# Transposing attention probabilities with VectorE and DMA instead of TensorE, keys stored even first

## Chip, cores and metric

The kernel runs on one core of a Trainium2 chip. The metric is the device time of one execution in microseconds (us), the median of several runs. The engines are named as in the profile: PE is TensorE's matmul and PEld its weight load, DVE is VectorE, ACT is ScalarE, POOL is GpSimd, SP is SyncE, which here only issues DMAs.

## The reference

The input is eight sequences of 512 tokens with 256 features, in float32. Each goes through a layer norm, a two-layer transformer of local attention and a gated feed-forward, half of its output added; then a recurrence over the tokens; then the same norm and transformer again. All of it is float32. What the change touches is the attention:

```python
def local_attention(q, k, v):
    ...
    bk, bv = (look_around(bk), look_around(bv))
    ...
    sim = jnp.einsum('bhwid,bhwjd->bhwij', bq, bk)
    ...
    mask = (i < j) | (i > j + WINDOW) | (j == -1)
    sim = jnp.where(mask, -jnp.finfo(sim.dtype).max, sim)
    attn = jax.nn.softmax(sim, axis=-1)
    out = jnp.einsum('bhwij,bhwjd->bhwid', attn, bv)
    return out.reshape(b, h, n, d)
```

There are 8 heads of 64 features. A window is 128 queries; they see the keys of their own window and of the one before it. The mask leaves each query its own key and the 128 before it. The first window has no window before it.

## The kernel before

**Tiles and loops.** `sequence(b)` lays out the work of one sequence. It calls `attention` and `feed_forward` four times each (two passes, two layers), with the recurrence in between. Each attention loops over four windows `w` of 128 tokens, and within a window over two groups `g` of four heads. So there are 8 x 4 x 4 = 128 windows and 256 groups.

**One window.** `h.turn` (L665) transposes the tokens, `qk` (L717) and `v` (L804) project them, VectorE and GpSimd apply the rotary tables, and `qk.turn` (L828) transposes queries and keys into `qT` and `kT`. Then, for each group:

- `sc` (L868) makes the scores, with queries on the partitions and keys along the free dimension. Queries 0 to 63 see 192 keys, queries 64 to 127 see 192 keys that begin 64 later; the first window has 128 keys.
- `least` (L911, VectorE) adds the mask, writes `pr` and finds the minimum of the negated scores; `exp` (L923, ScalarE) makes exponentials and their sum, one head at a time. `recip` (L936 or L938) and `shares` (L944) divide by the sum, two heads at a time, on VectorE or GpSimd.
- `pr.turn` (L970) transposes the probabilities on TensorE, 64 x 64 at a time, into PSUM, since `po` needs the keys on the partitions. `pr.copy` (L629, the line of every plain copy) brings them into `prT`.
- `po` (L1007) multiplies them with the values; `po.copy` and `po.add` (L1051) write `oT`.

After both groups `py` (L1058) projects the window's output and adds it to `x`. In the feed-forward, `hs.shift` issues two or three DMAs for each window on SP (L1085, L1086, L1088) that move `x` from SBUF to SBUF with half of the features shifted by one token; `h2T` and `gate` (L1151) and `down` (L1242) are its large matmuls.

**Order.** The order of instructions is fixed when the program is built. Every piece of work is a node with its engine or a choice of engines, a cost in ns, the nodes it depends on, and the buffers that it takes and frees. `Scheduler.run` repeatedly puts down the node that could start first by these costs. The table `EARLY` advances or delays kinds of nodes, and `VARIED` varies the choice in stretches of 5000 ns of the plan. Up to three sequences (`lane`) are under way at once, so that one sequence's attention lies beside another's feed-forward. Where a node has two engines, the plan chooses. A node's `tail` is the time after its end at which its result counts as there; for DMAs it stands for the transfer.

Each engine executes its instructions in this order and waits at each for semaphores. SP's queue is one of them: a DMA that waits holds up those behind it. The buffers around the change are six of `pr` (two heads each) and two of `prT` (one group each).

Of the kernel before, what the change touches and what calls it, by code (L numbers as in the profile page):

```python
# [15 lines left out]
P = 128  # L16
# [9 lines left out]
GATE = 64  # L26
NH1 = 2 * NFC * P + GATE + REM
DS = 64
# [4 lines left out]
NLV = 7  # L33


def shape_constants():
# [18 lines left out]
    key = j + i // DH * DH  # L55
    amask = np.where((key > i + P) | (key < i), -NEG, 0.0)
    j = np.arange(P)[None, :]
    amask = np.concatenate([amask, np.where(j > i, -NEG, 0.0)], 1)
# [56 lines left out]
def t_pool(n, spread=False):  # L115
# [6 lines left out]
    "XT6": 200,  # L122
    "_full_quad": 850,
    "_full_rows": 350,
    "_quad_full": 400,
    "_quad_rows": 450,
    "_rows_full": 500,
    "_rows_quad": 650,
    "_table": -250,
    "base.x": -700,  # L130
    "base.y": 50,
    "base.z": -550,
    "below": -250,
    "block": 1000,
    "bx": 500,
    "bx.copy": -450,
    "bx6": 1000,
    "bx6.copy": -1000,
    "cross.mask": 2000,
    "down": -300,  # L140
# [4 lines left out]
    "gram": -50,  # L145
    "gram.copy": -750,
    "h.copy": -1650,
    "h.edge": 2100,
    "h.turn": 200,
    "h2T": -800,  # L150
    "hn": 350,
    "hn.turn": 250,
    "hs.rstd": -1350,
    "hs.stats": 100,
    "hs.zero": -400,
    "k.scale": 2350,
    "keys": -200,
    "keys.copy": -300,
    "kq": 5100,
    "kq.copy": -1000,  # L160
    "last": 200,
    "last.gelu": -650,
    "least": -250,
    "norm 0": 100,
    "norm 1": 400,
    "ones": 2100,
    "po": 3300,
    "po.add": 50,
    "po.copy": 100,
    "pr.copy": -250,  # L170
    "pr.turn": 150,
# [3 lines left out]
    "qk.add": -100,  # L175
    "qk.copy": 100,
# [3 lines left out]
    "qk.swapped": 2800,  # L180
    "qk.turn": 5050,
    "recip": 950,
    "remains": 650,
    "rest": -200,
    "rope": -2950,
    "sc": 2350,
    "sequence 4": 350,
    "shares": -50,
    "start": 1000,
    "tv": 2350,  # L190
    "u": 5500,
    "u.copy": -100,
    "v": -50,
    "value": 150,
    "w": 4650,
    "w.add": 350,
    "x.ffn": 200,
    "x.rstd": -1900,
    "x.scale": -500,
    "x.stats": 500,  # L200
    "xbx": 2650,
    "xbx.t": 500,
    "xbx6": 1000,
    "y": 300,
    "z.rstd": -400,
    "z.scale": 50,
    "z.stats": 5600,
    "zT": -450,
    "zero": -1000,
    "zn.rstd": -1850,  # L210
    "zn.scale": -350,
    "zn.stats": -500,
    "zn.turn": 4500,
# [6 lines left out]
    11539, 59206, 52431, 7169, 51312, 47193, 35081, 54701, 2496, 7793, 6049, 56177, 10364, 34536,  # L220
    8294, 4310, 20154, 19168, 52227, 29170, 16540, 21667, 50441, 20648, 28762, 21176, 51225, 49241,
    45956, 34971, 21009, 28142, 19477, 38168, 5557, 12352, 7023, 53196, 6017, 32604, 32616, 33833,
    43497, 35592, 8, 9511, 36946, 21011, 40384, 28542, 18616, 35469, 46717, 3648, 49052, 34713,
    26816, 29204, 8404, 4647, 15343, 36844, 570, 21424, 12355, 42492, 50428, 45178, 54350, 17920,
    13395, 135, 39989, 44533, 2549, 22957, 29261, 17027, 29544, 14357, 27402, 53285, 13020, 11910,
    26247, 40152, 22117, 30422, 46544, 22999, 49636, 47593, 30197, 3179, 35589, 32132, 42056, 18356,
    57054, 3385, 45135, 14935, 20770, 32612, 13353, 15733, 35692, 48376, 37702, 12678, 33060, 54960,
    27803, 54969, 53369, 31335, 34476, 36715, 13, 17472, 3933, 49344, 40320, 43761, 51808, 53819,
    30473, 58888, 28378, 53574, 53586, 34808, 30271, 11754, 5097, 46663, 4587, 12477, 2842, 20974,
    22949, 16164, 56345, 59752, 37818, 42810, 36514, 28003, 38920, 15614, 32190, 14889, 45329,  # L230
    56333, 3909, 22135, 44005, 49596, 54630, 11534, 50699, 55304, 13694, 14380, 32785, 48251, 51975,
    59596, 39815, 34672, 26684, 43342, 49501, 38504, 13035, 9055, 59153, 49831, 29616, 8451, 2950,
    5921, 10921, 22426, 31491, 10417, 40901, 35295, 21598, 37874, 47623, 56332, 58977, 50639, 51395,
    14345, 21523, 1611, 59581, 38356, 9024, 8797, 9600, 33490, 20077, 18908, 39770, 12624, 0, 51302,
    12996, 28627, 14230, 30261, 45539, 33994, 58844, 55888, 53070, 40769, 41472, 42381, 21824,
    25505, 26825, 37644, 26704, 31501, 49830, 52837, 21763, 24330, 27631, 47626, 31160, 32421,
    20990, 43125, 47451, 26149, 56263, 41669, 38285, 29128, 53275, 59120, 363, 15861, 23553, 38689,
    16, 59208, 8741, 59992, 24971, 2133, 29045, 13059, 56697, 49647, 42350, 46546, 32101, 980,
    58623, 42263, 42129, 58230, 58436, 55171, 53628, 11325, 17446, 17234, 26564, 12471, 44487,
    47246, 47905, 19512, 6228, 20309, 9884, 23474, 21539, 12749, 53397, 58236, 36711, 21477, 28615,  # L240
    11585, 23822, 4616, 960, 14012, 19245, 52408, 9606, 51939, 36194, 40143, 58969, 31327, 21363,
    19023, 20707, 24836, 4653, 46695, 9517, 40252, 20970, 35385, 8326, 20484, 11202, 51312, 9682,
    42952, 35195, 31373, 29093, 31724, 58081, 5082, 52637, 24194, 57630, 47639, 14785, 25712, 17698,
    27876, 35732, 43008, 43338, 18992, 8751, 5850, 25733, 15460, 31028, 26546, 27345, 36488, 44056,
    33295, 58977, 39749, 29184, 25121, 23756, 33811, 26536, 2260, 15160, 321, 39968, 25191, 31222,
    45604, 48604, 7672, 56893, 14684, 26720, 30312, 41919, 57072, 2421, 44875, 34765, 3604, 10279,
    45490, 35361, 22716, 21175, 46557, 5008, 49647, 1355, 7859, 39941, 43761, 4026, 49030, 9539,
    56965, 8358, 3988, 59899, 58021, 13265, 53954, 9411, 13889, 26300, 5547, 22515, 925, 22821,
    35389, 36309, 3233, 50482, 32683, 44192, 45433, 54698, 24152, 37273, 3714, 29516, 35158, 19134,
    31173, 30908, 46863, 51249, 42973, 41570, 7558, 58198, 43105, 36002, 53169, 27713, 15508, 57450,  # L250
    13353, 45327, 20959, 21312, 25608, 23768, 55045, 27334, 58634, 20168, 34664, 55665, 6316, 39132,
    11849, 10070, 18798, 46877, 11811, 49462, 58565, 1501, 28373, 7960, 55865, 56429, 52621, 1403,
    19983, 51522, 6552, 248, 6935, 6388, 4871, 4789, 20877, 23567, 24542, 21112, 42445, 40535,
    41468, 43567, 1697, 53106, 45256, 50440, 21162, 41824, 59524, 4758, 53095, 48105, 39745, 19805,
    15895, 4145, 51961, 47869, 41251, 39860, 1162, 32717, 5615, 59674, 43307, 49529, 2408, 1126,
    6903, 26424, 10998, 1128, 11983, 31727, 294, 20411, 37533, 25779, 45123, 39019, 22071, 17092,
    35693, 44717, 33182, 15800, 26669, 36844, 32178, 27395, 16355,
# [189 lines left out]
def macaron_kernel(ctx: ExitStack, tc: tile.TileContext, a: dict, out: bass.AP):  # L447
# [21 lines left out]
    def both_of(*vals):  # L469
# [14 lines left out]
        "pr": buffers("pr", 6, [P, 8 * DH]),  # L484
        "prT": buffers("prT", 2, [P, 4, 4, DH]),
# [9 lines left out]
        "s8": buffers("s8", 8, [P, 8]),  # L495
# [23 lines left out]
    def load_x(b, w=None):  # L519

        if not w:
            lane[b], first_x[b] = Val("lane"), Val("x")
        own = slice(0, NW) if w is None else slice(w, w + 1)
        if w == 0 and b >= 2:
            taken[b] = node("lane.take", (b, -NW - 1), "SP", 0.0, lambda e: None, takes=[lane[b], first_x[b]], tail=0.0)
        order[0] += 1
        n = node(
            "load.x",
            (-1, order[0]) if b < 2 else (b, (w or 0) - NW),
            "SP",  # L530
            1500.0 if w is None else 450.0,
            lambda e: dma(first_x[b].ap[:, own, :], a["x"][b].rearrange("(w p) d -> p w d", p=P)[:, own, :]),
            [taken[b]] if b in taken else [],
            takes=[] if w or b in taken else [lane[b], first_x[b]],
            uses=[first_x[b]] if w or b in taken else [],
            tail=3600.0 if w is None else 2900.0,
        )
        L["x", b] = [n] * NW if w is None else [*L.get(("x", b), []), n]
# [67 lines left out]
    def sequence(b):  # L606
# [62 lines left out]
        def attention(x, l, ready):  # L669
# [3 lines left out]
            n_qk = n_v = n_k = None  # L673
            for w in range(NW):
# [6 lines left out]
                    [ready[w], L["ident"]],  # L681
# [3 lines left out]
                )  # L685
                n_h = copy(
# [129 lines left out]
                qT, oT = Val("qT"), Val("oT")  # L816
# [4 lines left out]
                def turn(pts=pts, turned=turned):  # L821
                    out = both_of(*pts)
                    for i in (1, 0):
                        rot = turned[i][0].ap
                        for g in range(HEADS // 2):
                            for r in range(2):
                                rows, at = slice(r * DH, (r + 1) * DH), ((1 - i) * 4 + g) * DH
                                nc.tensor.transpose(  # L828
                                    out[:, r, at : at + DH], rot[rows, g * P : (g + 1) * P], ident[rows, rows]
                                )  # L830
# [6 lines left out]
                    takes=[*pts, kT[w], qT, oT],  # L837
# [21 lines left out]
                outs = []  # L859
                half = lambda r: slice(r * DH, (r + 1) * DH)  # L860
                for g in range(2):

                    sc, prT = [Val("ps"), Val("ps")], Val("prT")
                    prs, sts = [Val("pr"), Val("pr")], [Val("s8"), Val("s8")]
# [1007 lines left out]
```

## Time and profile before

| what | value |
|---|---|
| time, median of 3 runs | 2645.85 us (2645.41 to 2647.25) |
| span of the profiled execution | 2645.8 us |
| instructions in the profile | 77025 |
| mean granted TensorE clock | 1.000 |
| transposes of queries and keys (L828), busy | 89.0 us, 2048 records |
| `po` (L1007), busy | 198.1 us, 7168 records |
| table loads of ScalarE at L923, L1173, L1212 | 97, 72 and 26, 1283 ns each |
| DMA issues of `hs.shift`, L1085 / L1086 / L1088 | 128 / 128 / 96 |
| data moved by DMA | 44.69 MB, mean 17 GB/s |

The profile has one execution. Busy times are unions of an engine's records; matmuls are pipelined, so that records of TensorE overlap and the sum of their durations is larger than the busy time. A row of a group gives busy time, mean duration of one, then the idle time of the engine just before such instructions and what ended it. A float32 matmul leaves two records in some groups. Idle time of an engine that the others do not wait for costs nothing.

### The profile page before, as it was taken

The numbers are of one execution on the slowest core, as the hardware profiler recorded it, in microseconds if no ns is written. First come the engines' busy times: TensorE is split into PE (matmuls) and PEld (weight loads), VectorE is DVE, ScalarE is ACT, GpSimd is POOL, SyncE is SP. The second block draws the span as 40 slices with busy tenths as digits, with TensorE's granted clock in tenths as the row PEclk, the third lists the DMA queues.
The fourth block names the chain that finished last, engine by engine and source line by source line (L and its number), as shares of the span: only waits on it lengthen the run. The fifth ranks groups of instructions, "written<-read, shape, count | busy, mean of one in ns | idle before, by whom it ended". The sixth has DMA issues, their size and how long they took to land.

```text
span 2645.8 us, 77025 instructions
## 1 busy us (share of the span) xinstructions
PE 2610.2 (99%) x30608; PEld 1961.5 (74%) x30608; DVE 1968.5 (74%) x5827; ACT 1647.9 (62%) x4328; POOL 1434.5 (54%) x2045
## 2 busy tenths in 40 slices
PE   8999999999999999999999999999999999999998
PEld 5777777677777777777777777777777777776776
DVE  7776776867878767877877678787677867867755
ACT  4666667655667756665566666667557665555754
POOL 8655464546565455654644466375445754546533
PEclk9999999999999999999999999999999999999999
DMA  5000000000100000000000001000001000000000
GB/s 186 10 8 10 17 8 16 6 8 8 34 7 10 9 11 28 8 10 7 19 23 9 8 10 30 6 10 9 7 8 32 11 8 10 22 7 6 14 9 17
DMA packets 59231, 44.69 MB, mean 17 GB/s; under 512 B 8140, under 2 KB 56440, under 8 KB 58872
## 3 DMA queue, kind: packets, MB, share of 16 engines
q1 hardware_dynamic: 58872, 39.77, 5.0%
q8 instruction: 241, 3.95, 0.6%
q14 instruction: 118, 0.97, 0.1%
HBM read 18.79 MB, written 4.19 MB: 9 GB/s over the span
## 4 chain that ended last, share of the span: by engine, by line
PE 66%; DVE 3%; ACT 2%; POOL 1%; issue 1%; DMA 0%; SPq 0%; DVEq 0%; ACTq 0%; POOLq 0%
PE ps L1151 16%; PE ps L717 12%; PE ps L1242 7%; PE ps L804 6%; PE ps L1058 6%; PE ps L1007 4%; PE ps L868 4%; PE ps L970 3%; PE ps L665 2%; PE ps L828 2%; PE ps L1255 1%; PE ps L1387 1%; PE ps L1498 1%; PE ps L1483 1%; ACT pr L923 0%
## 5 line engine op out<-in xcount | busy, mean ns | idle before, releaser
L1151 PE MATMUL ps<-h2T,w 128*128 128x256 f32 (+1 forms) x2816 | 651.5, 381 | 3.2 <-ACT h2T L1129 1.4
L1151 PEld LDWEIGHTS ps<-h2T,w 128*128 128x128 f32 (+1 forms) x2816 | 518.6, 188 | 121.9 <-issue 29.4
L717 PE MATMUL ps<-wqkv,hT 128*128 128x512 f32 x1024 | 487.5, 601 | 1.9 <-DMA wqkv<-in_wqkv_dram 1.8
L923 ACT ACTIVATE pr<-pr,s 128x192 f32<-128x192 f32 (+1 forms) x1024 | 439.8, 432 | 64.5 <-DVE s L911 61.2
L753 POOL TENSOR_TENSOR st<-st,powc 128x8 f32<-128x8 f32 x256 | 439.6, 1717 | 21.3
L911 DVE CUSTOM_DVE_ANT_0 pr<-ps,amask,st 128x192 f32<-128x192 f32 (+1 forms) x1024 | 353.8, 395 | 31.1 <-PE ps L868 28.1
L944 POOL TENSOR_TENSOR pr<-pr,s 128x384 f32<-128x384 f32 (+1 forms) x313 | 243.1, 787 | 202.4 <-DVE s L936 188.3
L717 PEld LDWEIGHTS ps<-wqkv,hT 128*128 128x128 f32 x1024 | 185.5, 191 | 160.1 <-issue 140.6
L1192 DVE SCALAR_TENSOR_TENSOR gT<-ps,b,gl 128x256 f32<-128x256 f32 x320 | 152.0, 482 | 195.5 <-PE ps L1151 167.1
L1242 PE MATMUL ps<-w,gT 128*128 128x256 f32 x1280 | 291.4, 380 | 0.0
L1242 PEld LDWEIGHTS ps<-w,gT 128*128 128x128 f32 x1280 | 241.5, 190 | 48.6 <-issue 16.3
L736 ACT ACTIVATE tmp<-ps 128x512 f32<-128x512 f32 x256 | 152.1, 596 | 195.8 <-DVE rot L761 134.6
L938 POOL TENSOR_TENSOR s<-s,powc 128x2 f32<-128x2 f32 x174 | 122.8, 707 | 278.7 <-ACT pr L923 276.1
L629 ACT COPY prT<-ps 128x512 f32<-128x512 f32 (+1 forms) x322 | 157.8, 542 | 151.1 <-PE ps L970 148.4
L1058 PE MATMUL ps<-wo,oT 128*128 128x256 f32 x1024 | 243.4, 380 | 0.5 <-DVE s L911 0.3
L804 PE MATMUL ps<-wqkv,hT 128*128 128x512 f32 x512 | 240.6, 594 | 0.1
L761 DVE TENSOR_TENSOR rot<-ps,rt 128x512 f32<-128x512 f32 x256 | 175.1, 686 | 74.4 <-PE ps L717 65.3
L1058 PEld LDWEIGHTS ps<-wo,oT 128*128 128x128 f32 x1024 | 191.2, 190 | 46.9 <-issue 16.1
L1173 ACT ACTIVATE gl<-ps,b 128x256 f32<-128x256 f32 x320 | 142.9, 474 | 108.4 <-PE ps L1151 100.2
L1007 PE MATMUL ps<-prT,v 64*64 64x128 f32 (+1 forms) x7168 | 198.1, 247 | 3.3 <-DVE prT L629 2.1
L868 PE MATMUL ps<-kT,qT 64*64 64x128 f32 (+1 forms) x7168 | 193.1, 250 | 4.2 <-issue 2.1
L923 ACT ACTIVATION_READ_ACCUMULATOR pr<-pr,s 128x1 f32 x1024 | 193.7, 189 | 0.0
(124 smaller groups left out, 4420.7 us busy)
## 6 DMA issues: line engine op xcount, KB each, us to landing
hs<-x SPq DMA_DIRECT2D x128, 64.0 KB
hs<-x SPq DMA_DIRECT2D x128, 63.5 KB
base<-in_x_dram SPq DMA_DIRECT2D x8, 512.0 KB
out_dram<-base SPq DMA_DIRECT2D x32, 128.0 KB
w<-in_w_dram SPq DMA_DIRECT2D x6, 640.0 KB
x<-in_x_dram SPq DMA_DIRECT2D x28, 128.0 KB
wqkv<-in_wqkv_dram SPq DMA_DIRECT2D x2, 1024.0 KB
hs<-x SPq DMA_DIRECT2D x96, 0.5 KB
```

The source lines that it names most:

```text
L717: nc.tensor.matmul(pp.ap, hT[w].ap[:, c * P : (c + 1) * P], wqkv[:, c, i * INNER : (i + 1) * INNER], start=(c == 0), stop=(c == 1),)
L753: nc.gpsimd.tensor_tensor(ss, ss, powc[:, 0:HEADS], ALU.pow)
L761: nc.vector.tensor_tensor(heads(rot.ap), heads(pp.ap), tab, ALU.mult)
L804: nc.tensor.matmul(pv.ap, hT[w].ap[:, c * P : (c + 1) * P], wqkv[:, c, 2 * INNER : 3 * INNER], start=(c == 0), stop=(c == 1),)
L868: nc.tensor.matmul(sc[par].ap[half(c), k * 4 * DH + at : k * 4 * DH + at + keys.stop - keys.start], qT.ap[half(par), 2 * g + k, half(c)], ...
L911: nc.vector.tensor_tensor_reduce(out=pr(k, nj), in0=sc.ap[:, k * 4 * DH : k * 4 * DH + nj], in1=amask[:, 0:nj] if w else amask[:, 3 * DH : ...
L923: nc.scalar.activation(pr(k, nj), pr(k, nj), AF.Exp, bias=st.ap[:, k : k + 1], scale=-1.0, accum_out=st.ap[:, 2 + k : 3 + k],)
L944: (nc.vector if e == "DVE" else nc.gpsimd).tensor_tensor(both, both, st.ap[:, 4:6].unsqueeze(2).to_broadcast([P, 2, nj]), ALU.mult)
L1007: nc.tensor.matmul(po[r].ap[half(par), k * P + first : k * P + first + cols * DH], v[j].ap[half(r), hd * DH : (hd + 1) * DH], prT.ap[half( ...
L1058: nc.tensor.matmul(py.ap[:, 0:D], oT.ap[:, c, :], wo[:, c, :], start=(c == 0), stop=(c == INNER // P - 1))
L1151: nc.tensor.matmul(dst.ap[0:rows, 0 : 2 * P], w1[:, kc, col : col + rows], h2T.ap[:, kc, :], start=(kc == 0), stop=(kc == 1),)
L1242: nc.tensor.matmul(py.ap[:, 0:D], gT.ap[:, at : at + P], w2[:, c, :], start=(c == 0), stop=False)
```

## The change

The probabilities are no longer transposed by TensorE. VectorE transposes them in place, in blocks of 32 x 32, and DMAs then move the blocks from `pr` to `prT`, SBUF to SBUF. Four things go with it.

- The keys in `kT` are stored with the even keys of each 64 first, then the odd ones. `qk.turn` writes them so: position 32 v + k holds key 2 k + v. The mask is laid out in the same order by `paired`.
- `pr` is now one buffer for all 8 heads of a window, cut in 32-key blocks; there are three, taken at `qk.turn`. `prT` holds a whole window too. One `recip` serves the four heads of a group.
- After `shares`, one flip for each group transposes all blocks of four heads. When both groups are flipped, two `pr.move` nodes on SP issue the moves, 12 DMAs for a window and 6 for the first one. Each takes 32 partitions, two neighbouring 32-key blocks and 8 heads: partition k of block m goes to partition 2 k + m of a half of `prT`, which puts the keys back in order. `po` of both groups waits for them.
- The tables `EARLY` and `VARIED` have new numbers, which give all engines a new order; each sequence takes its lane by a node of its own; the `h.turn` of one attention depend on each other in order; the space kept for DMA descriptors is 256.

```diff
+BLK = 32
...
+def paired(j):
+
+    return j // DH * DH + j % BLK * 2 + j % DH // BLK
...
-    key = j + i // DH * DH
+    key = paired(j) + i // DH * DH
...
-    amask = np.concatenate([amask, np.where(j > i, -NEG, 0.0)], 1)
+    amask = np.concatenate([amask, np.where(paired(j) > i, -NEG, 0.0)], 1)
...
-    "po": 3300,
...
-    "pr.copy": -250,
-    "pr.turn": 150,
+    "pr.out": 1850,
...
-        "pr": buffers("pr", 6, [P, 8 * DH]),
-        "prT": buffers("prT", 2, [P, 4, 4, DH]),
+        "pr": buffers("pr", 3, [P, 3 * DH // BLK, HEADS, BLK]),
+        "prT": buffers("prT", 2, [P, 2, P // BLK, HEADS, BLK]),
...
-        "s8": buffers("s8", 8, [P, 8]),
+        "s8": buffers("s8", 5, [P, 16]),
...
-                    [ready[w], L["ident"]],
+                    [ready[w], L["ident"], n_h0],
...
+                                dst = out[:, r, at : at + DH]
                                 nc.tensor.transpose(
-                                    out[:, r, at : at + DH], rot[rows, g * P : (g + 1) * P], ident[rows, rows]
+                                    dst.rearrange("p (v k) -> p k v", v=2) if i else dst,
+                                    rot[rows, g * P : (g + 1) * P],
+                                    ident[rows, rows],
                                 )
...
-                    takes=[*pts, kT[w], qT, oT],
+                    takes=[*pts, kT[w], qT, oT, prs],
...
+                            pr = lambda hd=4 * g + 2 * k + par, nb=nb, prs=prs: prs.ap[:, 0:nb, hd, :]
+                            cut = lambda t: t.rearrange("p (m i) -> p m i", i=BLK)
...
+                            nc.vector.reciprocal(st.ap[:, 8:12], st.ap[:, 4:8])
...
+                            both = prs.ap[:, 0:nb, 4 * g + 2 * k : 4 * g + 2 * k + 2, :]
+                            by = st.ap[:, 8 + 2 * k : 10 + 2 * k].unsqueeze(1).unsqueeze(3).to_broadcast([P, nb, 2, BLK])
+                            (nc.vector if e == "DVE" else nc.gpsimd).tensor_tensor(both, both, by, ALU.mult)
...
-                    def turn_pr(pts=pts, prs=prs, w=w):
-                        for h in range(4):
-                            for n in range(2 if w else 1):
-                                for r in range(2):
-                                    lo = DH + h % 2 * 3 * DH + (n * P - r * DH if w else 0)
-                                    at = (h * 2 + n if w else h) * DH
-                                    nc.tensor.transpose(
-                                        pts[r].ap[:, at : at + DH],
-                                        prs[h // 2].ap[half(r), lo : lo + P],
-                                        ident[half(r), half(r)],
-                                    )
...
+                    def flip(prs=prs, nb=nb, g=g):
+                        own = prs.ap[:, 0:nb, 4 * g : 4 * g + 4, :]
+                        nc.vector.transpose(own, own)
+
+                    flips.append(dve("pr.flip", 60.0 + 1.1 * 4 * nj, flip, [*n_w, *flips], takes=[] if g else [prT], uses=[prs]))
+
+                def moves(q, w=w, prs=prs, prT=prT):
+                    for m in range(3 if w else 1 + q // 2):
+                        n, u = divmod(m + (q // 2 if w else 2), 2)
+                        dma(
+                            prT.ap[u * DH : (u + 1) * DH, n, q].rearrange("p h i -> p (h i)"),
+                            prs.ap[q * BLK : (q + 1) * BLK, 2 * m : 2 * m + 2].rearrange("k m h i -> k m (h i)"),
                         )
...
+                moved = [
+                    node(
+                        "pr.move",
+                        prio(),
+                        "SP",
+                        (6 if w else 2 + 2 * r) * 430.0,
+                        lambda e, r=r, moves=moves: [moves(q) for q in (2 * r, 2 * r + 1)],
+                        flips,
+                        uses=[prs, prT],
+                        tail=2300.0,
+                    )
+                    for r in range(2)
+                ]
...
+                            out = po[r].ap[half(par), k * P + first : k * P + first + cols * DH]
                             nc.tensor.matmul(
-                                po[r].ap[half(par), k * P + first : k * P + first + cols * DH],
+                                out.rearrange("p (q i) -> p q i", i=BLK),
                                 v[j].ap[half(r), hd * DH : (hd + 1) * DH],
-                                prT.ap[half(r), h, n : n + cols, :],
+                                prT.ap[half(r), n // 2, q : q + 2 * cols, hd, :],
...
-                        [*tps, *(vals[j] for j in blocks)],
+                        [*moved, *(vals[j] for j in blocks)],
...
-        for pr in pools["pr"]:
-            for edge in (slice(0, DH), slice(7 * DH, 8 * DH)):
-                nc.gpsimd.memset(pr[:, edge], 0.0)
...
-    nc = bacc.Bacc("TRN2", target_bir_lowering=False, num_devices=1)
+    nc = bacc.Bacc("TRN2", target_bir_lowering=False, num_devices=1, dynamic_dma_scratch_size=256)
```

## The prediction

> **What bounds the kernel now.** I read the page's busy shares and slices first, then the chain of work that ended last, then the groups of instructions with shapes kept apart, then the timelines of TensorE and of the DMA queue.
>
> ```profile
> PE 2610.2 (99%) x30608; PEld 1961.5 (74%) x30608; DVE 1968.5 (74%) x5827; ACT 1647.9 (62%) x4328; POOL 1434.5 (54%) x2045
> ...
> PE   8999999999999999999999999999999999999998
> ...
> PEclk9999999999999999999999999999999999999999
> ```
>
> TensorE is busy in 99% of the span at the full granted clock, in every slice alike. Of 2645.8 us it is idle in 35.6. By windows, 11.2 us of that lie in the first 100 us and 6.6 in the last 46; some 18 are left for the 2500 us between. So there is no wait to remove: only TensorE work can be saved.
>
> ```profile
> PE 66%; DVE 3%; ACT 2%; POOL 1%; issue 1%; DMA 0%; SPq 0%; DVEq 0%; ACTq 0%; POOLq 0%
> ```
>
> The chain says the same: other engines end a wait in 6% of it.
>
> ```profile
> L970 PE MATMUL ps<-sq,pr 64*128 64x64 f32 x3584 | 144.1, 225 | 3.1 <-DVE pr L944 0.7 <-POOL pr L944 0.7 <-DVE tmp L767 0.7
> L629 ACT COPY prT<-ps 128x512 f32<-128x512 f32 x239 | 131.1, 596 | 106.2 <-PE ps L970 103.5 <-ACT tttb L1378 0.8 <-ACT pr L923 0.7
> L629 DVE COPY prT<-ps 128x512 f32<-128x512 f32 x145 | 95.1, 685 | 35.2 <-PE ps L970 34.3
> L944 DVE TENSOR_TENSOR pr<-pr,s 128x384 f32<-128x384 f32 x148 | 87.7, 611 | 2.3 <-POOL s L938 0.6
> L629 ACT COPY prT<-ps 128x256 f32<-128x256 f32 x83 | 26.7, 386 | 44.9 <-PE ps L970 44.9
> L944 DVE TENSOR_TENSOR pr<-pr,s 128x256 f32<-128x256 f32 x51 | 23.2, 465 | 0.9
> L629 DVE COPY prT<-ps 128x256 f32<-128x256 f32 x45 | 17.3, 419 | 17.1 <-PE ps L970 17.0
> ```
>
> L970 is the transposition of probabilities that goes away; its copies stand on ScalarE and VectorE.
>
> **Removed from TensorE.** The 144.1 us of L970 overlap with their neighbours, because each matmul of 225 ns is started long before the last one ends. What the removal frees is the distance from start to start:
>
> ```profile
> 1035.37 2.32 PE L1242 MATMUL ps<-w,gT 128*128 128x256 f32 x10
> 1037.63 1.21 PE L970 MATMUL ps<-sq,pr 64*128 64x64 f32 x32
> 1038.67 0.66 PE L828 MATMUL ps<-sq,rot 64*128 64x64 f32 x16
> ...
> 1056.37 0.66 PE L970 MATMUL ps<-sq,pr 64*128 64x64 f32 x16
> 1056.95 3.29 PE L1151 MATMUL ps<-h2T,w 128*128 128x256 f32 x14
> ```
>
> 32 of them hold the engine from 1037.63 to 1038.67, 1.04 us; 16 before a full matmul, 0.58. At 0.55 us per 16 (34.4 ns each) 3584 give 123 us; the bounds are 32.5 ns (116 us) and 36.5 ns, the mean over all stretches of L970 up to whatever follows (131 us). A change between full-array and partial-array matmuls costs extra: the ten matmuls of L1242, 0.215 us apart elsewhere, hold 2.26 us here, 0.11 too many. I counted such changes in the order of instructions of both programs: 558 before, 563 after. The stretches with L970 often also hold L828, which remains, so nothing comes from there. 2645.8 - 123 = 2523.
>
> **Added to TensorE.** No matmul is added. The first matmuls of each window's `po` now wait for the semaphores of twelve DMAs instead of two copies; the order shows 835 waits that need an instruction of their own, 665 before, at 51 ns each in the trace: 170 x 51 ns = 9 us at most, nothing if they pass while matmuls drain. I take 4. The 1024 key transposes of L828 write every 32nd word of PSUM in turn. No row shows that; L828's 89.0 us for 2048 bound it: 0 to +44 us if the half concerned took twice as long. I take 0, by the plain L828 row, since the same words are written, only in another order.
>
> **VectorE.** It loses the copies (95.1 + 17.3 = 112.4), 120 of 338 reciprocals at 159 ns (19, one now serves four heads), 55 of its 148 large `shares` at 593 ns (33, the order puts them on GpSimd), and 28 of 157 additions at 694 ns (19). It gains 192 flips of 768 elements per partition and 64 of 512, an operation no row shows. Low end, by the copies: (685 - 419) / 256 = 1.04 ns per element, so 951 and 685 ns, 226 us in all. By `shares`, (611 - 465) / 128 = 1.14 ns, 1049 and 757 ns, 250 us. High end, if it ran at half the rate, 500 us. I take 235, nearer the copies (one input, one output). 1968.5 - 183 + 235 = 2020 us, 80% of 2523, against 74% now: no bound. ScalarE loses 157.8 us of copies and 28 of 195 table loads at 1283 ns, and stands near 1460 us; GpSimd loses 136 of 174 reciprocals and takes over `shares` and additions, and stays at 1433.
>
> [...]
>
> **The moves.** Each window (four 128-row blocks, two layers, two passes, eight sequences: 128) gets 12 DMAs, or 6 for the first block of each attention: 96 x 12 + 32 x 6 = 1344 of 64 KB, issued on SP. The nearest row is the shift of `hs`, also SBUF to SBUF:
>
> ```profile
> 401.97 0.51 SPq L1085 DMA_DIRECT2D hs<-x  x1
> 402.53 0.62 SPq L1086 DMA_DIRECT2D hs<-x  x1
> 403.20 0.94 SPq L1088 DMA_DIRECT2D hs<-x  x1
> ```
>
> One issue to the next takes 0.56 us at L1085 (64 KB) and 0.67 at L1086; the stores to DRAM (352 ns median) give 0.41. The packets of one L1085 begin 1.16 us after its issue and are all done at 1.50, over many engines at once; the 127 rows of L1086 go one after another, 23.5 ns apart, to 4.99 us. 64 packets of 1 KB take 46 to 53 ns each: 1344 x 64 x 50 ns / 16 = 270 us per engine, a tenth of the span. SP's issues, 1344 x 0.56 = 753 us and 128 shifts of 2.2, fill under half. So neither is a throughput bound.
>
> What can cost is lateness. All twelve moves of a window stand between its last flip and its first `po`: 12 x 0.56 = 6.7 us and 1.0 to land, 7.7. The program's own plan, which fixes the order, allows 12 x 0.43 + 2.3 = 7.5. By L1790's price it is 5.9, by L1086's 9.1. Between a window's last `sc` and its first `po`, the new order puts a median of 17.9 us of TensorE work (counted from the order, each matmul at its start-to-start time above). The steps between, each without queueing, are four `least` (1.7), the rest of the exponentials (0.9), `recip` and `shares` (1.0), the last flip (1.0) and the moves (7.7): 12.3 us. So the cover exists, but it is not large. Queued behind a waiting move on SP are the shifts: 86 times the order puts moves right after a shift, whose three issues hold SP for 2.2 us where the plan has 0.5. At 2.2 of 20.7 us per window a tenth of 128 windows meets one, for 1 us on average, half of it exposed: 6 us. Each DMA also waits for the one eight places ahead of it to land; 8 x 0.56 covers 1.5 us, not an L1086's 4.4, and that is in the same 1 us. At the start the first moves queue behind weight loads that keep the DMA engines full from 10 to 36 us: 0 to 10 us, I take 4. If the cover is gone, a microsecond of lateness costs 128 us.
>
> **The rest of the diff.** New tables of the plan set a new order of all work. Its worth is bounded by TensorE's idle time: the 18 us in the middle can be gained, the second rival is the loss; I take 0. The extra order among `h.turn` binds instructions of one engine, the memsets left out are twelve short ones of GpSimd at the start, and the smaller scratch space issues nothing: 0.
>
> **Sum:** 2645.8 - 123 + 4 + 6 + 4 = 2537 us. The runs' median, 2645.85, is the profiled span, so nothing is added around it.
>
> **The rivals.** First: flips at half rate (500 us). VectorE then stands at 2285 us, 90% of the span, and each window's path is 2 us longer; a quarter of it exposed gives 2537 + 64 = 2600. For it: nothing in the profile shows a transpose. Against: one-input rows run near 1.04 ns per element.
>
> Second, slower than before: SP's issues set the pace of each window. Lateness per window is 10.5 moves x (price - 0.43); fully exposed, 1344 x (p - 0.43) eats the 109 us from p = 0.51 on, half exposed from 0.59. At L1086's 0.67 and half exposed: 2537 + 161 = 2698. For it: the price of L1085 lies between these points. Against: the faster landing (1.0 for 2.3 planned) pays back 1.3 us of each window, and the plan drops the 3300 ns by which `po` was advanced, so `po` now yields to other ready work, which is slack.
>
> Third: the moves do not spread over the DMA engines, as L1086 does not. 64 packets at 46 ns in a row, 1344 times, is 3960 us. L1085's 128 rows spread; 32 and 64 rows are not shown. [...]
>
> Fourth: TensorE has the time but nothing ready to fill it, and idles it away: 2646.
>
> **How the numbers follow.** Forecast, 2505 to 2590: 0.70; its low end is 2645.8 - 131 and a little for a shorter wait elsewhere, its high end the 44 us of strided writes. Better than that, 0.03. Flips at half rate, 0.10. SP's pace, 0.13. No spread, 0.02. No change, 0.02. A change of 0.2% (5 us) is about what can be told from none here. Faster is 0.70 + 0.03 + 0.10 = 0.83, same 0.02, slower 0.15. The likeliest case gives 2537; a range of 2502 to 2620 takes in the half-rate flips and leaves the slower cases out.
>
> **What would show it.** TensorE still at 97% or more of a shorter span, L970 and the copies of `prT` gone, VectorE near 2020 us, flips near 0.95 us, moves 0.5 to 0.6 us apart on SP and landed within 2 us. Idle time of TensorE before `po`, released by DMA `prT`, beyond 15 us speaks for the second rival; a flip above 1.5 us for the first. I am wrong if TensorE's busy time does not fall by about 120 us.

## The result, and the profile after

The changed kernel takes 2729.34 us, the median of 4 runs (2729.08 to 2732.07), where the kernel before takes 2645.63 (2644.73 to 2647.25) beside it: a ratio of 1.0315, interval 1.030 to 1.033. It is slower by 84 us; the forecast was 109 us faster. The profiled execution has a span of 2727.3 us at a mean granted clock of 0.982.

First the busy shares and the slices of the changed kernel.

```profile
PE 2575.4 (94%) x27024; PEld 1893.8 (69%) x27024; DVE 2009.3 (74%) x5669; ACT 1479.3 (54%) x3999; POOL 1428.2 (52%) x1980
...
PE   7998999999999999999999999999999999999988
```

TensorE has 3584 records fewer, and yet its busy time fell by 34.8 us only (2610.2 before), while its share fell from 99% to 94%. The other engines are where the prediction had them: VectorE 2009 us (2020 foretold), ScalarE 1479 (1460), GpSimd 1428 (1433). The chain of work that ended last names what is new.

```profile
PE 75%; DMA 7%; SPq 6%; DVE 6%; ACT 3%; issue 2%; POOL 1%; DVEq 0%; ACTq 0%; POOLq 0%
```

DMA and SP's queue had 0% of the chain before; together they now have 13%. The groups, with shapes kept apart, say at which line TensorE waits.

```profile
L1009 PE MATMUL ps<-prT,v 64*64 64x128 f32 x3584 | 222.4, 296 | 98.9 <-DMA prT<-pr 78.8 <-issue 8.6 <-DVE s L923 4.3
...
L977 DVE STREAM_TRANSPOSE pr<-pr 128x768 f32<-128x768 f32 x192 | 185.8, 970 | 11.9 <-POOL pr L960 8.1
...
L977 DVE STREAM_TRANSPOSE pr<-pr 128x512 f32<-128x512 f32 x64 | 45.1, 706 | 3.1 <-POOL pr L960 1.0
```

L1009 is `po`. Its first form alone has 98.9 us of idle time ahead of it; 78.8 of them end when a move into `prT` lands. Of the kernel before, the same row:

```profile
L1007 PE MATMUL ps<-prT,v 64*64 64x128 f32 x3584 | 180.9, 275 | 3.3 <-DVE prT L629 2.1 <-ACT prT L629 0.8 <-issue 0.2
```

The flips at L977 cost 970 and 706 ns, 230.9 us in all.

Here is one window. First SP's queue, then TensorE, then all engines in three stretches of it (columns: length, then busy time of PE, PEld, DVE, ACT and POOL, each with its records, then PEclk, the granted clock in parts of full speed, the DMA engines' share, and GB/s).

```profile
1074.81 0.52 SPq L1087 DMA_DIRECT2D hs<-x  x1
1075.37 0.68 SPq L1088 DMA_DIRECT2D hs<-x  x1
1076.09 0.92 SPq L1090 DMA_DIRECT2D hs<-x  x1
1077.12 7.67 SPq L984 DMA_DIRECT2D prT<-pr  x12
```

```profile
1082.91 0.72 PE L840 MATMUL ps<-sq,rot 64*128 64x64 f32 x16
1085.83 2.91 PE L1009 MATMUL ps<-prT,v 64*64 64x128 f32 x61 [2.20 <-DMA prT<-pr]
1088.44 0.42 PE L882 MATMUL ps<-kT,qT 64*64 64x128 f32 x1
```

```profile
1080.00:1085.50 5.50, 3.63 (x30) 2.86 (x28) 2.02 (x5) 2.02 (x4) 1.27 (x1) 1.00 0.41 101
1085.50:1088.90 3.40, 3.07 (x73) 3.10 (x77) 0.85 (x2) 0.02 (x1) 0.00 (x0) 0.50 0.09 22
1088.90:1095.00 6.10, 6.10 (x49) 4.19 (x42) 4.41 (x22) 5.51 (x19) 2.23 (x4) 1.00 0.00 1
```

A shift holds SP for 2.3 us, then twelve moves go out in 7.67 us, 0.64 each; the last is out at 1084.79 and `po` starts 1.04 us later, at 1085.83, after 2.20 us in which TensorE had nothing. The semaphores show that its first matmul waits for the eleventh move, which lands at 1085.70; the twelfth lands only at 1086.31. Then a second cost appears that the forecast did not have: for the next 3.4 us the granted clock is 0.50, and `po` itself runs slowly (61 matmuls in 2.91 us; after the wait that ends at 1010.64, at full clock, 61 take 1.92). Between the first and the last matmul the clock is halved for 95.6 us (0 before).

A third change is small but everywhere: instructions that only wait for semaphores, between the matmuls of `po`, for the moves that are still to land. They stand in the stream of weight loads (PEld). The first line is of the kernel before, the second of the changed one (durations in ns: least, median, most).

```profile
L1007 PEldq EVENT_SEMAPHORE  x169: 51/51/51, 33.1 to 2607.3; - x169
```

```profile
L1009 PEldq EVENT_SEMAPHORE  x584: 51/51/3020, 39.8 to 2693.3; - x195
```

The account, from TensorE's records. A matmul holds the engine from its start to the next one's start; idle time is taken out of this and stands apart, counted from the first matmul to the last:

| part | us |
|---|---|
| L970 gone | -127 |
| TensorE's idle time, 23.4 to 141.3 (of it before `po`, 3.3 to 104.1) | +118 |
| matmuls in the half-speed stretches, against the same matmuls at the rate of before | +42 |
| the other matmuls, held longer (`po` +24, L840 +8, the rest in parts below 5) | +50 |
| sum (the spans differ by +81.5; the first matmul starts 1.6 us sooner) | +83 |

So all that L970 held is gone, and 210 us come back: waits, most of them for the moves, the halved clock after them, and matmuls held longer.

### The profile page after: what moved, and what is told of

It reads as the page before. It is cut to its first block, busy times and chain, and to the rows that moved or that the text cites. A ratio compares the mean times of both kernels' runs of the same rounds, so it can differ in the third digit from the quotient of the medians.

```text
span 2727.3 us, 71864 instructions
## 1 busy us (share of the span) xinstructions
PE 2575.4 (94%) x27024; PEld 1893.8 (69%) x27024; DVE 2009.3 (74%) x5669; ACT 1479.3 (54%) x3999; POOL 1428.2 (52%) x1980
## 4 chain that ended last, share of the span: by engine, by line
PE 75%; DMA 7%; SPq 6%; DVE 6%; ACT 3%; issue 2%; POOL 1%; DVEq 0%; ACTq 0%; POOLq 0%
PE ps L1153 20%; PE ps L728 13%; PE ps L1244 8%; PE ps L1009 7%; PE ps L1060 7%; PE ps L815 6%; SPq L984 5%; PE ps L882 5%; DMA prT<-pr 4%; PE ps L675 2%; DMA hs<-x 2%; PE ps L840 2%; DVE pr L923 1%; ACT pr L935 1%; PE ps L1389 1%
## 5 line engine op out<-in xcount | busy, mean ns | idle before, releaser
L1153 PE MATMUL ps<-h2T,w 128*128 128x256 f32 (+1 forms) x2816 | 655.6, 383 | 8.4 <-DVE gT L1194 3.4
L1153 PEld LDWEIGHTS ps<-h2T,w 128*128 128x128 f32 (+1 forms) x2816 | 519.4, 189 | 124.9 <-issue 21.7
L960 POOL TENSOR_TENSOR pr<-pr,s 128x384 f32<-128x384 f32 (+1 forms) x368 | 290.1, 807 | 418.7 <-DVE s L949 370.6
L728 PE MATMUL ps<-wqkv,hT 128*128 128x512 f32 x1024 | 490.8, 604 | 2.3 <-DMA wqkv<-in_wqkv_dram 2.1
L935 ACT ACTIVATE pr<-pr,s 128x192 f32<-128x192 f32 (+1 forms) x1024 | 439.1, 431 | 73.4 <-DVE s L923 67.4
L764 POOL TENSOR_TENSOR st<-st,powc 128x8 f32<-128x8 f32 x256 | 434.1, 1696 | 21.3
L1009 PE MATMUL ps<-prT,v 64*64 64x128 f32 (+1 forms) x7168 | 237.9, 265 | 104.1 <-DMA prT<-pr 82.9
L1009 PEld LDWEIGHTS ps<-prT,v 64*64 64x64 f32 x7168 | 210.1, 145 | 134.9 <-issue 76.4
L648 POOL TENSOR_SCALAR st<-st 128x1 f32<-128x1 f32 (+1 forms) x192 | 49.7, 259 | 390.8 <-DVE st L1101 226.9
L815 PE MATMUL ps<-wqkv,hT 128*128 128x512 f32 x512 | 245.7, 604 | 2.2 <-DVE tmp L778 2.2
L977 DVE STREAM_TRANSPOSE pr<-pr 128x768 f32<-128x768 f32 (+1 forms) x256 | 230.9, 904 | 15.0 <-POOL pr L960 9.1
L1060 PEld LDWEIGHTS ps<-wo,oT 128*128 128x128 f32 x1024 | 192.0, 191 | 54.1 <-issue 20.1
L639 ACT COPY oT<-ps 128x256 f32<-128x256 f32 x232 | 86.5, 373 | 235.7 <-PE ps L1009 233.3
## 6 DMA issues: line engine op xcount, KB each, us to landing
hs<-x SPq DMA_DIRECT2D x128, 63.5 KB
```

What stands on the lines that cost most here:

```text
L728: nc.tensor.matmul(pp.ap, hT[w].ap[:, c * P : (c + 1) * P], wqkv[:, c, i * INNER : (i + 1) * INNER], start=(c == 0), stop=(c == 1),)
L764: nc.gpsimd.tensor_tensor(ss, ss, powc[:, 0:HEADS], ALU.pow)
L815: nc.tensor.matmul(pv.ap, hT[w].ap[:, c * P : (c + 1) * P], wqkv[:, c, 2 * INNER : 3 * INNER], start=(c == 0), stop=(c == 1),)
L935: nc.scalar.activation(pr(), pr(), AF.Exp, bias=st.ap[:, h : h + 1], scale=-1.0, accum_out=st.ap[:, 4 + h : 5 + h],)
L960: (nc.vector if e == "DVE" else nc.gpsimd).tensor_tensor(both, both, by, ALU.mult)
L977: nc.vector.transpose(own, own)
```

## The experiments

Theory A: the moves come late because SP needs about 0.65 us for each, one after another, where the plan has 0.43; TensorE waits before `po`, and the halved clock and the semaphore instructions follow from that. Theory B, as the rival: what costs is in TensorE's own work, above all the key transposes that now write every 32nd word, or in the new order.

**Fewer moves of the same kind.** One move of three is kept in every full window; the rest of `prT` is cleared once at the start.

```diff
-                    for m in range(3 if w else 1 + q // 2):
+                    for m in [1] if w else [0]:
...
+        for t in pools["prT"]:
+            nc.gpsimd.memset(t, 0.0)
```

> The changed kernel in its order with 4 of 12 moves for each window (one for each block of 32 queries); the other probabilities are not moved, and prT is cleared once at the start. Theory A: 4 x 0.65 + 1.1 = 3.7 us against 7.5 planned, idle time before po under 15 us, the clock at full speed nearly throughout, 2530 to 2570 us, near what the removal of the transposes alone was worth. Theory B: above 2650 us.

2559.52 us (one run), span 2557.4. Its shares:

```profile
PE 2508.0 (98%) x27024; PEld 1847.0 (72%) x27024; DVE 2005.7 (78%) x5669; ACT 1475.7 (58%) x3999; POOL 1431.9 (56%) x1982
```

All instructions of the compute engines are those of the changed kernel (GpSimd has two clearings more), in the same order; only moves are missing. TensorE's idle time falls to 39.0 us, before `po` to 3.4, the half-speed time to 13.7. TensorE's busy time alone falls by 67 us though it does the same work: the clock and most of what `po` is held longer, too, hang on the moves. Theory A is right about the cause of the waits before `po`. B is left with the 18 us by which matmuls are still held longer than before (7 of them at L840), and with 16 us more of idle time elsewhere than before `po` (35.6 against 20.1).

**The same data in eight moves instead of twelve.** The score columns are laid out so that two pieces of 64 keys that go to the same partitions lie side by side, and travel as one DMA of 128 KB.

```diff
-        "prT": buffers("prT", 2, [P, 2, P // BLK, HEADS, BLK]),
+        "prT": buffers("prT", 2, [P, P // BLK, 2, HEADS, BLK]),
...
-                    for m in range(3 if w else 1 + q // 2):
...
+                    c = q // 2
+                    if w:
+                        dma(into(c, 0, 2), part(c, 2))
+                        dma(into(1 - c, c, 1), part(2 * (1 - c), 1))
...
```

> Same plan and order as the changed kernel, correct output, but a full window is moved in 8 DMAs instead of 12: the scores' columns and prT are laid out so that two 64-key pieces of one query block go in one DMA with 2 KB pieces. Theory A (the loss is lateness: SP needs 0.65 us for each move, 12 x 0.65 + 1.1 us to land = 8.9 us where the plan allows 7.5): 8 x 0.65 + 1.1 = 6.3 us, so TensorE's idle time before po falls from 104 us to under 30, the half-speed time of its clock from 98 us to under 40, and the time from 2729 to 2590 to 2630 us. Theory B (the loss comes from elsewhere in the change: semaphore waits on TensorE, strided writes of keys, VectorE's load, the new order itself): within 20 us of 2729. Should the price of an issue grow with its bytes, A would give some 2690 us.

2593.89 us, ratio 0.9803 (0.9786 to 0.9819): it beats both kernels. Its shares and its `po`, then the issues of its moves (L996 is the move of 128 KB, L997 that of 64 KB):

```profile
PE 2525.5 (97%) x27024; PEld 1858.1 (72%) x27024; DVE 2006.1 (77%) x5669; ACT 1476.7 (57%) x3999; POOL 1426.2 (55%) x1980
...
L1022 PE MATMUL ps<-prT,v 64*64 64x128 f32 (+1 forms) x7168 | 207.1, 249 | 22.5 <-DMA prT<-pr 13.6
```

```profile
L996 SPq DMA_DIRECT2D prT<-pr x384: 537/597/1544, 48.4 to 2556.1; - x192
L997 SPq DMA_DIRECT2D prT<-pr x384: 537/597/1810, 49.0 to 2556.7; - x192
```

Twice the bytes cost the same 597 ns of SP. So the price is one for each of these DMAs, and four DMAs fewer in a window are worth 135 us. Idle time before `po` falls from 104.1 to 22.5 us with the bytes unchanged. The bytes are not free in the transfer: by its semaphore, a move of 128 KB has landed 2.62 us after its issue began (median), one of 64 KB in the changed kernel 2.13.

**The strided writes alone.** The kernel before, with the keys even first in the key transposes only and the mask left as it was.

```diff
+                                dst = out[:, r, at : at + DH]
...
-                                    out[:, r, at : at + DH], rot[rows, g * P : (g + 1) * P], ident[rows, rows]
+                                    dst.rearrange("p (v k) -> p k v", v=2) if i else dst,
+                                    rot[rows, g * P : (g + 1) * P],
+                                    ident[rows, rows],
```

> The kernel before with the keys of qk.turn written even first, then odd, and nothing else; the mask is left in the old order, so other keys are masked. If a transpose that writes every 32nd word in turn costs nothing: 2645 +- 3 us and 225 ns for each matmul of qk.turn. If it costs the 3.8 ns by which the mean distance of these matmuls grew in the changed kernel: +4 to +10 us. If it takes twice as long: +44 us.

2645.85 us against 2646.11, ratio 1.0001 (0.9992 to 1.0010), 10 and 13 runs. The strided writes cost nothing that this run can tell (a matmul of `qk.turn` takes 225 ns and holds TensorE for 36.8 ns in both kernels); the 8 us by which L840 is held longer in the changed kernel come from something else, perhaps from its neighbours in the new order, which was not shown.

**Half of the moves from ScalarE's queue.** To tell SP's pace from a late flip or a late landing, the second six of each window's twelve moves were issued by ScalarE at the same place in the order.

```diff
-                def moves(q, w=w, prs=prs, prT=prT):
+                def moves(q, dma=nc.sync.dma_start, w=w, prs=prs, prT=prT):
...
-                        lambda e, r=r, moves=moves: [moves(q) for q in (2 * r, 2 * r + 1)],
+                        lambda e, r=r, moves=moves: [moves(q, (nc.sync, nc.scalar)[r].dma_start) for q in (2 * r, 2 * r + 1)],
```

> Second half of each window's moves (six of twelve) issued from ScalarE's queue, the first half from SP's; order and plan unchanged. Theory A (the issues of the moves, 0.65 us one after another on one queue, are what comes late): the last move is issued some 6 x 0.65 = 3.9 us earlier in every window, so TensorE's idle time before po falls from 101 us to 40 or less, and the time to 2570 to 2640; median from first move's issue to po 6 us or less (9.4 now). Theory C (the flips or the landing come late, not the issues): po starts no sooner, and ScalarE, which now holds 672 issues and waits for the flips, costs something: 2730 or more. Between: ScalarE's own work is delayed by the moves (some 0.6 x 672 = 400 us more on an engine that is 54% busy) and gives back part: 2640 to 2730, with new waits before exp or copies of ScalarE.

2832.73 us, ratio 1.0696 (1.0667 to 1.0724): slower again by 103 us, which no theory had in its numbers except C's open end. But the place is not C's: idle time before `po` falls from 104.1 to 32.0 us, as A says, and 191 us of idle time now stand elsewhere (37 before that edit). In the list of waits (engine, line, released by: us in total, times, longest) ScalarE has a new one:

```profile
ACT gl L1175 <- DMA prT<-pr: 106.0, 24, 7.8
...
ACT tmp L747 <- DMA prT<-pr: 68.0, 15, 6.9
...
ACT hT L639 <- DMA prT<-pr: 62.3, 15, 7.8
ACT kT L639 <- DMA prT<-pr: 56.0, 12, 8.8
ACT v L639 <- DMA prT<-pr: 53.3, 12, 8.5
```

346 us in these five: activations and copies of ScalarE that stand behind its issues. The timeline of ScalarE shows one such case.

```profile
1019.60 4.47 ACTq L984 DMA_DIRECT2D prT<-pr  x5
1024.17 0.58 ACT L639 COPY v<-ps 128x512 f32<-128x512 f32 x1 [4.24 <-DMA prT<-pr]
```

TensorE then waits for ScalarE: of its 39.1 us before `sc`, 36.0 end with a copy of ScalarE, and of its 60.5 before L1153, 32.8 end with ScalarE's work and 27.1 with VectorE's. With two queues the twelve issues of a window take 5.9 us from first to last (median of the 96 full windows), not half of the 8.1 of one queue (median of the 90 that go out unbroken). That is not because each issue gets slower: from one to the next it is 643 ns on SP (median) while ScalarE issues and 642 while it does not, and 652 on ScalarE. ScalarE begins 1.03 us after SP (median), and each queue has some longer steps. Where both begin within 25 ns of each other, the whole takes 4.1 us at best. So the second queue saves some 2 of 8.1 us of a window's issues, and what ScalarE loses is larger: the 346 us above are 2.7 us for each of the 128 windows.

**Eight moves, half of them from ScalarE's queue.** The same edit on the kernel with eight moves.

> Eight larger moves instead of twelve, as in the merged kernel (2594 us), and the second half of them issued from ScalarE's queue. Theory A: four issues on each queue, as late as with four moves in all, which gave 2559.5; so 2555 to 2580. If ScalarE's blocked time costs more than the 22 us of waits that are left: 2594 or more.

2673.04 us, ratio 1.0104 (1.0089 to 1.0119), against 2593.89 without it. Theory A's 2555 to 2580 was wrong; the other branch, 2594 or more, came true. There was little left to gain before `po` (22.5 to 19.8 us), and ScalarE, in the five largest such lines of its list of waits, stands 204.7 us behind the landing of a move.

**The shifts from ScalarE's queue.** To find the share of the collisions between shifts and moves, the shifts of `hs` left SP: on the changed kernel, and on the kernel with eight moves.

```diff
-                def shift(e, w=w):
+                def shift(e, w=w, dma=nc.scalar.dma_start):
```

> The 128 shifts of hs (three DMAs each, two for the last block) issued from ScalarE's queue instead of SP's; moves unchanged on SP. Of 103 us of waits before po, 39 us follow directly on a shift's issues. If these collisions are a cause of their own, about 39 us of idle time and as large a share of the clock's loss go: 2650 to 2690. If the waits come from the pace of the twelve moves alone and the shifts only happen to lie there: 2715 to 2735. The prediction's figure (6 us for the collisions) would give 2723.

> Eight larger moves on SP, and the shifts of hs issued from ScalarE's queue. 22 us of waits before po are left in the merged kernel; if a third or more follows shifts: 2570 to 2588. If shifts don't matter: 2590 to 2598. ScalarE's queue delayed by the shifts' waits: above 2600.

2866.61 us (ratio 1.0838, 1.0821 to 1.0854) and 2757.96 (1.0419, 1.0403 to 1.0434). Both are slower than with the shifts on SP, the first beyond every range that was expected, and neither answers the question. ScalarE, in the list of waits of the first (twelve moves), is held by the shifts:

```profile
ACT kT L639 <- DMA hs<-x: 25.6, 5, 6.3
...
ACT hT L639 <- DMA hs<-x: 22.3, 5, 7.2
ACT pr L935 <- DMA hs<-x: 21.7, 7, 3.8
```

Exponentials (L935) are among them, so that some probabilities come later, and idle time before `po` grows to 128.7 and 45.7 us; how much of this growth comes from the exponentials was not shown. What share of the changed kernel's waits the collisions on SP have stays open: of its 103 us before `po`, 39 follow directly on a shift's issues, but what would be left of them without the shifts was not shown.

All kernels in one table. Idle is TensorE's, in us, from the profiled execution; half speed is the time with the granted clock at 0.5. Both are counted from the first matmul to the last.

| kernel | time | idle | of it before `po` | half speed |
|---|---|---|---|---|
| before | 2645.6 | 23.4 | 3.3 | 0.0 |
| changed, 12 moves in a window | 2729.3 | 141.3 | 104.1 | 95.6 |
| 8 moves | 2593.9 | 56.5 | 22.5 | 20.5 |
| 4 moves (data left out) | 2559.5 | 39.0 | 3.4 | 13.7 |
| 6 on SP, 6 on ScalarE | 2832.7 | 223.5 | 32.0 | 184.3 |
| 4 on SP, 4 on ScalarE | 2673.0 | 113.3 | 19.8 | 61.4 |
| 12 moves, shifts on ScalarE | 2866.6 | 241.3 | 128.7 | 150.2 |
| 8 moves, shifts on ScalarE | 2758.0 | 167.6 | 45.7 | 78.5 |

In all kernels that transpose on VectorE, the time less the idle time and less half of the half-speed time lies between 2514 and 2551 us (for 8 moves, 2593.9 - 56.5 - 10.3 = 2527). The kernel before has 2622 by the same sum, and 2622 - 123 = 2499 was foretold: the work that is left is 15 to 52 us more than that, the matmuls held longer among it, and the waits make most of the difference between these kernels.

## Why the prediction was wrong

- **TensorE's saving: right for L970, too high in sum.** 123 us were foretold, with bounds of 116 and 131; L970 held the engine for 127 us without idle time, and they are gone. But the other matmuls were taken to stay as they were; even with four moves, where `po` hardly waits, they are held 18 us longer, and 109 are left of the saving.
- **VectorE and the flips: right.** 970 and 706 ns against 951 and 685 of the copies' rate; 230.9 us against 235, and VectorE is busy for 2009 us against 2020. Flips at half rate, the first rival, fell.
- **Strided key writes: right.** Priced at 0; the run of them alone shows none.
- **Spread over the DMA engines: right.** The third rival fell; a move does not run row by row: it has landed 2.13 us after its issue began (median of all 1344, by its semaphore), where 64 packets at 46 ns in a row would take 2.9 us alone. The profile before has no DMA of 32 or 64 rows, so the 0.02 given to this rival was the author's estimate.
- **Semaphore instructions: perhaps mis-sized.** At most 9 us by 170 of them; their number is right (835 against 665), but outside the half-speed stretches `po`'s matmuls are held 24 us longer. With 482 such instructions at `po` (8 moves) they are held 12 us longer, with 268 (4 moves) 4 us. The waits fall along with their number, so what the 584 of the changed kernel cost by themselves was not shown.
- **The moves: here it failed.** The step that failed is "12 x 0.56 = 6.7 us and 1.0 to land, 7.7", set against the plan's 7.5, and "So the cover exists, but it is not large". The 0.56 came from L1085. A move's issue takes 597 ns (median) and the next follows 0.642 us after its start (median; mean 0.682, since 55 steps take over 1 us): above the 0.56 of L1085 with as many bytes, and nearer to the 0.67 of L1086, which was read in one place and has a median of 0.717 over the run. So from the first issue of twelve moves to `po` it takes 9.4 us (median of the windows that waited), 1.7 more than the 7.7 and 1.9 more than the plan's 7.46. The wait for the DMA eight places ahead is not what slows them: the step from the eighth issue to the ninth is 0.696 us (median). The 1.0 to land came out right by luck: it was read from packets, and by its semaphore a move lands 1.53 us after its issue ends (median). `po` still starts 1.04 us after the last issue ends, because its first matmul does not need the last move: in 61 of the 79 waits it starts before that one has landed.
- **The cover: argued with the wrong statistic.** A median of 17.9 us of TensorE work between `sc` and `po` against a path of 12.3 without queueing says nothing of the windows below the median. 79 waits of over 0.1 us before `po` are what that leaves. The kernel with four moves shows that the cover would have served a path some 8 x 0.65 = 5.2 us shorter. Whether an order planned with 0.65 us for each move would have given the twelve enough cover, no run shows.
- **What a wait costs: not priced.** The 6 us for collisions and the second rival's 161 us counted the wait alone. Against the 127 us that are gone stand 118 of idle time, 42 of the halved clock that follows, and 50 of matmuls held longer.

The second rival was the right mechanism: its 2698 us, at 0.67 us a move and half exposed, is 31 us below the result, and its sign, idle time before `po` released by DMA `prT` beyond 15 us, is met by 82.9 us in TensorE's list of waits. That the number came so near is partly luck, since neither the halved clock nor the longer matmuls are in it. The arguments against it were too weak: the earlier start of `po` after the last issue (1.04 us for 2.3 planned) did pay back 1.3 us of a window, but 10.5 x (0.68 - 0.43) = 2.6 us were owed, and whatever slack the dropped advance of `po` gave did not cover the rest.

## What to carry to other kernels

A transfer that stands between two steps of a pipeline is priced first by the number of its DMAs times the issue price on one queue: here 597 ns for an issue of 64 or of 128 KB (median), and 0.64 us from one to the next of 64 KB, so that merging twelve into eight turned a loss of 3.2% into a gain of 2.0%. The price is read from a DMA of the same shape, not of the same size: in the changed kernel the three DMAs of a shift hold SP for 521 ns (64 KB), 677 (63.5 KB) and 920 (0.5 KB). An order that was planned with a lower price can spend the difference as waits of the engine that sets the time, and for TensorE a wait of 2 us can cost more than 2 us: here 2.20 us before `po` were followed by 3.41 us at a clock of 0.50. A second queue is not free where its engine has other work in order behind the issues: with six moves of a window on it, ScalarE stood 346 us behind them.

## What the hardware showed that was not expected

- SP's price of a DMA from SBUF to SBUF does not grow from 64 to 128 KB: 597 ns median both times. It does differ with the shape (521 ns at L1087, also 64 KB).
- The clock falls to half for 3.41 or 6.83 us after short waits. Of the 23 such stretches among the matmuls of the changed kernel, 20 begin at most 4.3 us after the start of a wait before `po` of 1.65 to 5.24 us, the other three after waits before other lines. All of them begin on one grid of 3.41 us, and in the 3.41 us before each TensorE was idle for 53% or more of the time (54% in the window shown above). At full clock, from 17.11 us on, where its record begins, only two intervals of this grid with more than half of their time idle (54 and 57%) were not followed by a fall. A whole interval without work was not needed: it stands ahead of only two of the 23 falls (58.07 and 2594.17 us).
- Two queues that issue at the same time hardly slowed each other: from issue to issue on SP it is 643 ns (median; mean 721) with issues of ScalarE beside it and 642 (667) without.
